# The passage between two decoder layers: order of the last batch's work, places of seven products, and one turning moved by a slot

## The chip, the cores and the metric

One core of one Trainium2 chip runs the whole kernel. Its engines work side by side, each through its own queue in order: TensorE (PE, with its weight loads shown as PEld), VectorE (DVE), ScalarE (ACT), GpSimd (POOL) and SyncE (SP), whose queue issues most transfers. An instruction that waits for another engine holds up everything behind it in its own queue. The metric is the device time of one execution in microseconds (us), lower is better.

## The reference

Two decoder layers over 32 batches of 100 tokens with 256 features, 16 heads of 16. Each layer is self-attention, cross-attention to 361 context rows per batch, and a feed-forward part, each followed by a residual and a normalisation without weights. All is in float32. Cut to what matters here:

```python
x = layernorm(x + L0_attn(x))                      # adds x once more inside
x = layernorm(x + L0_xattn(x, ctx, ctx, dist))     # scores - |scale| * log(dist + 1e-9)
x = layernorm(x + L0_ffn(x))
x = layernorm(x + L1_attn(x))
x = layernorm(x + L1_xattn(x, ctx, ctx))
x = layernorm(x + L1_ffn(x))                       # router, the best of 8 experts, times its share

def L0_ffn(x):
    xn = (x - mean) * rsqrt(var + 0.001) * ln_gamma + ln_beta
    w_q = clip(round(weight / (mean(abs(weight)) + EPS)), -1, 1)
    gamma = max(abs(xn))                           # over ALL batches and tokens
    xq = clip(xn * 128 / gamma, -128 + EPS, 128 - EPS)
    return (xq @ w_q) * (gamma * beta / 128)
```

The maximum `gamma` is taken over all batches. So the feed-forward part of layer 0, and with it all of layer 1, can start only when the last batch has passed layer 0's cross-attention.

## The kernel before

The attention part of both layers is one program written by hand in slots. `at(slot, place, do)` files a step under a slot and a place; `run_slots` then walks the slots in order and records every step, which fixes the order in each engine's queue. No scheduler moves anything afterwards.

A slot `s` consists of the scores of the unit two slots ahead (TensorE into the four score banks, then `centre` on DVE and POOL), place -1 and place 0, and then three turns of the unit one slot ahead (TensorE transposes the centred scores, ACT takes the exponential out of PSUM), each followed by places 1, 2 and 3. Last come the sums of the slot's own unit (weights times values). A unit is the self-attention of a batch or a quarter (four heads) of its cross-attention: five units, so five slots, per batch. There is only one set of score banks, so the next unit's scores wait until DVE has read the last ones. All other products go through four PSUM banks in turn, `bank(...)`.

Layer 0's cross-attention of batch b starts in slot 5b, so the last one, batch 31, in slot 155. Layer 1's starts in slot 183 + 5b, and its self-attention earlier: batches 0 to 3 in slots 173, 175, 177 and 179, batch 4 in slot 185. Between slots 160 and 182 lies what is called the passage here.

The last batch's chain in the passage: `normalised` (the transposes `r_n_x`, then on DVE a reciprocal and the product `o_x`), the turning of `o_x` (`r_x_ox`), `residual` (product `r_o_x`, then on DVE the sum and its statistics, on POOL the power -0.5), `centre_and_scale`, `layer_norm_scale`, `feed_forward_input` (`xn` and its largest magnitude into `absmax`), then `scale_of_all` in slot 164, place 3: a reduction of `absmax` on DVE, a transpose `r_gmax`, another reduction, a product `r_gamma` that spreads the result over 128 partitions, and the scales. `clipped` then makes `xq`, and `feed_forward` (`r_f`) gives the first rows of layer 1.

Beside it the passage makes 34 pieces. For each of batches 2 to 9 (`AHEAD`) three value products of layer 1's cross-attention (`r_v_ahead`, each two matmuls and an ACT copy) are made ahead into a stage and stored to DRAM; for batches 0 and 1 there are two key pieces (`r_k`) and three value pieces (`r_v`) each. `PASSAGE` lists the slot and place of each piece in this order. Behind the last piece of a batch SP issues the store of its values and the load of the context for the batch two further on.

For a batch of layer 1 from 4 on, self-attention has its scores in slot `early` - 2 and its sums in slot `late` = `early` + 1. In slot `late` + 1 follow `normalised` at place 0 (`r_n_s`, then `o_s` on DVE) and the turning of `o_s` at place 3 (`r_x_os`, two transposes, and an ACT copy). In slot `late` + 2 that copy goes into `residual` at place 2 (`r_o_s`). That slot begins with the scores of the next batch's self-attention.

Of the kernel before, what the change touches and what calls it, by code (L numbers as in the profile page):

```python
# [16 lines left out]
B, S, D, H, DH = 32, 100, 256, 16, 16  # L17
# [17 lines left out]
NO_TOKEN = 1000000  # L35
ROUND = 12582912.0
AHEAD = range(2, 10)
PASSAGE = ((160, 3), (160, 3), (160, 3), (161, 1), (162, 2), (162, 2), (163, 1), (163, 2), (163, 2), (163, 3), (164, 1), (164, 1),
           (164, 2), (165, 1), (166, 1), (167, 3), (167, 3), (167, 3), (169, 1), (169, 3), (171, 3), (171, 3), (173, 1),
           (174, -1), (174, 0), (175, 1), (176, -1), (176, 0), (177, 1), (178, -1), (178, 0), (179, 1), (180, -1), (180, 0))  # L40
LAYER = (0, SLOTS * B + 23)
COLUMNS = ("parity", "steps", "l0s_bq", "l0s_bk", "l0s_bv", "l0x_bq", "l0x_bk", "l0x_bv", "l1x_bq", "l1x_bk", "l1x_bv")
ROWS = ((("l0s_bo", D), ("l0x_bo", D), ("dscale", 1), ("ffn_g", D), ("ffn_b", D)),
# [21 lines left out]
def decoder_kernel(ctx: ExitStack, tc: tile.TileContext, a: dict, out: bass.AP):  # L65
# [7 lines left out]
    xnT = state.tile([P, NC2, B, S], F32, name="xnT")  # L73
# [7 lines left out]
    def layer_norm_scale(pool, src, eps, kind, tag):  # L81

        n = src.shape[0]
        st = pool.tile([n, 6], F32, tag="ln_st", name=f"st_{tag}")
        nc.vector.bn_stats(st, src)
        mv = pool.tile([n, 2], F32, tag=f"ln_mv_{kind}", name=f"mv_{tag}")
        nc.vector.bn_aggr(mv, st)  # L87
        rs = pool.tile([n, 1], F32, tag=f"ln_rs_{kind}", name=f"rs_{tag}")
        nc.gpsimd.tensor_scalar_add(rs, mv[:, 1:2], eps)  # L89
        nc.gpsimd.tensor_tensor(rs, rs, mhalf[:n], ALU.pow)  # L90
        return mv[:, 0:1], rs

    def centre_and_scale(dst, src, scale):
        nc.vector.tensor_scalar(dst, src, scale[0], scale[1], ALU.subtract, ALU.mult)

    with ExitStack() as att:
# [7 lines left out]
        def bank(tag):  # L104
            return ps_r.tile([P, 512], F32, tag="r", name=f"r_{tag}")

        def split(t, n):
            return t.rearrange("p (n s) -> p n s", n=n)
# [129 lines left out]
        def transpose_rows(src, kind, tag, dst=None):  # L238

            ps = bank(f"x_{kind}{tag}")[:, :NC2 * S]  # L240
            for k in range(NC2):
                nc.tensor.transpose(ps[:, k * S:(k + 1) * S], src[:, k * P:(k + 1) * P], ident[:S, :S])
            if dst is None:
                dst = w2.tile([P, NC2, S], F32, tag=f"xT_{kind}", name=f"xT_{kind}{tag}")
            nc.scalar.copy(dst, split(ps, NC2))
            return dst
# [35 lines left out]
        def normalised(avs, tag):  # L282


            psn = bank(f"n_{tag}")[:S].rearrange("p (h r) -> p h r", r=32)
            for g in range(NG):
                nc.tensor.transpose(psn[:, g * NG:(g + 1) * NG, :].rearrange("p h r -> p (h r)"), avs[:, g, :], ident)
            rc = sm.tile([S, H], F32, tag="rc", name=f"rc_{tag}")
            nc.vector.reciprocal(rc, psn[:, :, DH])
            o = w2.tile([S, H, DH], F32, tag="o", name=f"o_{tag}")  # L290
            nc.vector.tensor_tensor(o, psn[:, :, :DH], rc.unsqueeze(2).to_broadcast([S, H, DH]), ALU.mult)
            return o
# [6 lines left out]
        def residual(oT, w_o, y, weight, kind, tag):  # L299

            pso = bank(f"o_{kind}{tag}")[:S, :D]
            for k in range(NC2):
                nc.tensor.matmul(pso, lhsT=oT[:, k, :], rhs=w_o[:, k, :], start=(k == 0), stop=(k == NC2 - 1))
            nc.vector.scalar_tensor_tensor(y, y, weight, pso, ALU.mult, ALU.add)
            return layer_norm_scale(sm, y, 1e-05, kind, f"{kind}{tag}")
# [91 lines left out]
        def at(slot, place, do):  # L397
            plan.setdefault((slot, place), []).append(do)
# [68 lines left out]
        def starts(l, b):  # L467


            return LAYER[l] + SLOTS * b, LAYER[l] + (2 * b - 10 if b < 4 else SLOTS * (b - 4) + 2)  # L470
# [20 lines left out]
        def plan_passage():  # L491
# [17 lines left out]
            for load, of_batch in [ahead(b) for b in AHEAD] + [(live[1, b]["load"], live[1, b]["pieces"]) for b in range(2)]:  # L509
                n = len(loads)  # L510
                loads.append(load)
                pieces += [(f, None) for f in of_batch[:-1]] + [(of_batch[-1], n + 2)]
            assert len(pieces) == len(PASSAGE)
            for i in range(2):
                at(157 + i, 0, loads[i])
                at(157, 3, lambda i=i: nc.gpsimd.memset(stage[i][:, :, :, DH:], 1.0))
            for (slot, place), (f, then) in zip(PASSAGE, pieces):
                at(slot, place, f)
# [3 lines left out]
        def plan_batch(l, b):  # L522
            start, early = starts(l, b)
            t = live[l, b] = {}
            sx = f"l{l}x"
            tag = f"{l}_{b}"

            def keep(key, f):
                def do():
                    t[key] = f()  # L530
                return do
# [52 lines left out]
            def flat(o):  # L584
                return o.rearrange("p h d -> p (h d)")
# [24 lines left out]
            late = early + (b > 3)  # L610
            bursts.setdefault(late, []).append(steps[early].sums)
            at(early if b < 4 else early - 2, 0, keep("y_s", lambda: add_share(c[f"l{l}s_bo"], "s", b, tag)))
            at(late + 1, 0, keep("o_s", lambda: normalised(t["av_s"], f"s{tag}")))
            at(late + 1, 3, keep("oT_s", lambda: transpose_rows(flat(t["o_s"]), "os", tag)))
            at(late + 2, 2, keep("ln_s", lambda: residual(t["oT_s"], c[f"l{l}s_wo"], t["y_s"], 1.0 if l else 2.0, "s", tag)))
            at(late + 3, 2, lambda: centre_and_scale(xs[b], t["y_s"], t["ln_s"]))
            for g in range(NG):
# [6 lines left out]
            at(start + 7, 1, keep("ln_x", lambda: residual(t["oT_x"], c[sx + "_wo"], t["y_x"], 1.0, "x", tag)))  # L624
            at(start + 8, 1, lambda: centre_and_scale(xs[b], t["y_x"], t["ln_x"]))
            if l == 0:
                at(start + 8, 2, keep("ln_n", lambda: layer_norm_scale(sm, xs[b], 0.001, "n", f"n_{b}")))
                at(start + 9, 3, feed_forward_input)
                at(start + 11, 3, lambda: transpose_rows(t["xn"], "n", tag, dst=xnT[:, :, b, :]))
            else:  # L630
                at(start + 9, 0, keep("x3T", lambda: transpose_rows(xs[b], "m", tag)))
                first, n = group_of(b)
                r, steps_of_group = ROUTING[max(0, b - (B - 3))]
                at(start + r[0], r[1], router)
                if b == first + n - 1:
                    for do, (s, place) in zip((ranked, exponentials, ahead_of, counted, shares, rows_of), steps_of_group):
                        at(start + s, place, lambda do=do: do(first, n))
                    s, place = steps_of_group[-1]
                    for i in range(n):
                        at(start + s + i, place, lambda i=i: send(first + i))  # L640
# [9 lines left out]
        def group_of(b):  # L650

            if b >= B - 2:
                return b, 1
            first = b // GROUP * GROUP
            return first, min(GROUP, B - 2 - first)
# [51 lines left out]
        def send(b):  # L707
            nc.gpsimd.tensor_copy(place[:, b:b + 1], row[:, b:b + 1])
            scatter("regions", out=regions, out_offset=bass.IndirectOffsetOnAxis(ap=place[:, b:b + 1], axis=0),
                    in_=x_all[:, b, :])  # L710
# [97 lines left out]
        for l in range(2):  # L808
            for b in range(B):
                plan_batch(l, b)  # L810
            for b in range(0, B, 2):
                plan_pair(l, b)
# [196 lines left out]
```

## Time and profile before

| | us |
|---|---|
| median of 3 runs (lowest, highest) | 1762.18 (1759.08, 1764.57) |
| the profiled execution | 1765.71 |
| its span, first to last instruction | 1763.7 |
| layer 0, to the end of the last batch's `r_n_x` | 0 to 834.27 |
| passage, to layer 1's first cross-attention scores | 834.27 to 906.04 |
| start of layer 1's cross-attention, to batch 1's second scores | 906.04 to 934.02 |
| rest of layer 1 | 934.02 to 1664.30 |
| experts | 1664.30 to 1763.7 |
| granted TensorE clock, mean over the span | 0.986 of full |

Every row of an engine's timeline is one or more instructions of the same line that ran behind each other: the start, the time from the first start to the last end, the engine, the line of the kernel, the tiles written and read, and the count. In brackets stands how long the engine had been idle before it and what ended the wait. A product of two matmuls in float32 appears as four matmul records. Consecutive rows overlap by some 0.16 us, since the end of a matmul overlaps the start of the next, so costs are taken from start to start. Tiles that begin with `r_` are the PSUM banks of a product, `sc_` the score banks; buffer and batch numbers are left out of the names.

### The profile page before, as it was taken

How to read it: one execution, taken by the hardware profiler on the slowest of the kernel's cores; microseconds unless marked ns; L12 is line 12 of the kernel's file. 1: busy time of each engine (PE TensorE's matmuls, PEld its weight loads, DVE VectorE, ACT ScalarE, POOL GpSimd, SP SyncE). 2: the span in 40 equal slices, each digit the busy share in tenths (PEclk: the TensorE clock that was granted, in tenths of full speed). 3: DMA queues.
4: the chain of work that ended last, by engine and by line, in shares of the span. 5: the costliest groups of instructions: out<-in, count | busy, mean ns of one | idle time of the engine just before them, and what ended most of it. 6: DMA issues, size and time to landing. Idle time of an engine off the chain costs nothing. (4 is left out here: it accounts for less than half of the span.)

```text
span 1763.7 us, 52249 instructions
## 1 busy us (share of the span) xinstructions
PE 1691.6 (96%) x20801; PEld 1307.2 (74%) x20801; DVE 1292.9 (73%) x3784; ACT 910.5 (52%) x2252; POOL 1098.6 (62%) x1657
## 2 busy tenths in 40 slices
PE   7999999999999999999899999999999999999786
PEld 6777777777777777766667777777777777777575
DVE  4677777777778777777567887877768787777655
ACT  3455555555555555555445555555555555554354
POOL 1566666666666666666136668776767667775646
PEclk9999999999999999999999999999999999999888
DMA  4001332333233223200601132000000000010083
GB/s 153 20 21 30 80 76 52 84 80 76 56 84 81 71 57 84 76 25 22 209 20 46 54 102 64 19 20 19 28 19 15 24 19 28 31 32 18 18 249 117
DMA packets 64047, 104.90 MB, mean 59 GB/s; under 512 B 6107, under 2 KB 43485, under 8 KB 63678
## 3 DMA queue, kind: packets, MB, share of 16 engines
q1 hardware_dynamic: 59790, 94.44, 19.2%
q0 software_dynamic: 3584, 6.59, 1.2%
q8 instruction: 165, 2.70, 0.6%
q14 instruction: 76, 0.62, 0.1%
q10 hardware_dynamic: 432, 0.54, 0.1%
HBM read 61.32 MB, written 41.13 MB: 58 GB/s over the span
## 5 line engine op out<-in xcount | busy, mean ns | idle before, releaser
L364 POOL TENSOR_TENSOR pr<-pr,mx_x 100x361 f32<-100x361 f32 x992 | 767.0, 803 | 230.9 <-DVE mx_x L360 222.2
L375 ACT ACTIVATE pT_x<-r_t_x 120x400 f32<-120x400 f32 (+1 forms) x768 | 371.8, 504 | 305.7 <-PE r_t_x L374 304.8
L374 PEld LDWEIGHTS r_t_x<-ident,pr 100*120 100x120 f32 (+1 forms) x3072 | 314.1, 138 | 119.0 <-POOL pr L364 39.5
L374 PE MATMUL r_t_x<-ident,pr 100*120 100x100 f32 (+1 forms) x3072 | 384.1, 253 | 14.5 <-POOL pr L364 12.7
L360 DVE CUSTOM_DVE_ANT_0 pr<-sc_x,dist 100x361 f32<-100x361 f32 x512 | 244.6, 531 | 122.7 <-PE sc_x L277 113.7
L360 DVE CUSTOM_DVE_ANT_0 pr<-sc_x,zero 100x361 f32<-100x361 f32 x512 | 244.6, 530 | 76.6 <-PE sc_x L277 65.6
L277 PE MATMUL sc_x<-kT_x,qz_x 32*100 32x361 f32 x2048 | 222.4, 503 | 8.3 <-DVE mx_x L360 5.2
L89 POOL TENSOR_SCALAR rs_s<-mv_s 100x1 f32<-100x1 f32 x64 | 14.4, 225 | 293.8 <-DVE mv_s L87 264.6
L389 PE MATMUL r_a_x<-pT_x,v_cross 120*32 120x100 f32 (+1 forms) x6144 | 172.7, 253 | 0.0
L318 DVE TENSOR_REDUCE mx_s<-sc_s 100x16 f32<-100x1600 f32 x64 | 116.7, 1823 | 75.0 <-PE sc_s L277 75.0
L477 ACT ACTIVATE kT_x<-r_k,c_columns 128x361 f32<-128x361 f32 x128 | 72.1, 564 | 162.4 <-PE r_k L475 162.4
L389 PEld LDWEIGHTS r_a_x<-pT_x,v_cross 120*32 120x32 f32 (+1 forms) x6144 | 130.2, 110 | 23.9 <-ACT kT_s L424 2.2
L332 ACT ACTIVATE pT_s<-r_t_s 100x400 f32<-100x400 f32 x256 | 112.9, 505 | 33.3 <-PE r_t_s L331 31.0
L321 DVE TENSOR_TENSOR pr_s<-sc_s,mx_s 100x1600 f32<-100x1600 f32 x64 | 116.8, 1825 | 2.2
L331 PE MATMUL r_t_s<-ident,pr_s 100*100 100x100 f32 x1024 | 107.3, 251 | 0.3 <-DVE pr_s L321 0.3
L277 PEld LDWEIGHTS sc_x<-kT_x,qz_x 32*100 32x100 f32 x2048 | 68.3, 160 | 45.9 <-issue 13.9
L484 PE MATMUL r_v<-shared,ctx 128*120 128x256 f32 (+1 forms) x384 | 100.4, 384 | 0.0
L331 PEld LDWEIGHTS r_t_s<-ident,pr_s 100*100 100x100 f32 x1024 | 95.1, 130 | 5.8 <-ACT shared L486 0.7
L486 ACT COPY v_cross<-r_v 120x256 f32<-120x256 f32 x168 | 62.6, 373 | 57.5 <-PE r_v L484 57.5
L268 DVE SCALAR_TENSOR_TENSOR qz_x<-r_qx,qm_x_scale,qm_x_bias 128x400 f32<-128x400 f32 x64 | 37.6, 629 | 72.7 <-PE r_qx L257 72.7
L475 PE MATMUL r_k<-ctx,shared 128*128 128x361 f32 x256 | 89.6, 472 | 1.1 <-DMA ctx<-in_ctxT_dram 1.1
L475 PE MATMUL r_k<-ctx,c_l1x_wk 128*128 128x361 f32 x256 | 89.2, 471 | 0.0
(220 smaller groups left out, 2920.2 us busy)
## 6 DMA issues: line engine op xcount, KB each, us to landing
regions<-no_token SPq DMA_DIRECT2D x23, 1161.0 KB
ctx<-in_ctxT_dram SPq DMA_DIRECT2D x64, 361.0 KB
wb<-in_experts_dram SPq DMA_DIRECT2D x32, 257.0 KB
values_dram<-shared SPq DMA_DIRECT2D x8, 768.0 KB
v_cross<-values_dram SPq DMA_DIRECT2D x8, 768.0 KB
dist<-in_dist_dram SPq DMA_DIRECT2D x32, 141.0 KB
xb<-regions SPq DMA_DIRECT2D x32, 129.0 KB
x_all<-in_x_dram SPq DMA_DIRECT2D x32, 100.0 KB
```

Of the source, the lines that this page charges most:

```text
L277: nc.tensor.matmul(dst, lhsT=qz[rows, p, k, :], rhs=kT[rows, k, :], start=True, stop=True)
L318: nc.vector.tensor_reduce(mx, sg, AX.X, ALU.max)
L321: nc.vector.tensor_tensor(pr, sg, mx.unsqueeze(3).to_broadcast([S, NG, NG, S]), ALU.subtract)
L331: nc.tensor.transpose(pt[:, j, :], t["pr_s"][:, j, g, :], ident[:S, :S])
L332: nc.scalar.activation(t["pT_s"][:, g], pt, AF.Exp)
L360: nc.vector.tensor_tensor_reduce(pr[:, j, :SK], sc[:, j, :], bias, 1.0, LOWEST, ALU.add, ALU.max, mx)
L364: nc.gpsimd.tensor_tensor(pr[:, j, :SK], pr[:, j, :SK], mx.to_broadcast([S, SK]), ALU.subtract)
L374: nc.tensor.transpose(pt[:n, j, :], t["pr_x", g][:, j, k0:k0 + n], ident[:S, :S])
L375: nc.scalar.activation(t["pT_x", g][:n, i], pt[:n], AF.Exp)
L389: nc.tensor.matmul(av[32 * j:32 * j + 32, h, :], lhsT=t["v_x"][:n, i, head(part, j), :], rhs=t["pT_x", part][:n, i, j, :], start=(i == 0), ...
L475: nc.tensor.matmul(ps, lhsT=c[sx + "_wk"][:, k, m * P:(m + 1) * P], rhs=t["ctx"][:, k, :], start=(k == 0), stop=(k == NC2 - 1))
L484: nc.tensor.matmul(ps, lhsT=ctx_b[:, k, k0:k0 + n], rhs=c[sx + "_wv"][:, k, :], start=(k == 0), stop=(k == NC2 - 1))
```

## The change

Three edits, none of which alters a value that is computed:

- The places of the 34 pieces. Before, 13 of them stood in slots 160 to 164; now six do. From there on every piece takes a place that another had before, and the last seven go into slots 181 to 186, where there were none.
- For batch 30 alone (`b == B - 2`), `feed_forward_input` and the transposes of its result move two slots on, from 159 to 161 and from 161 to 163. On DVE its three instructions thereby come behind `o_x` of batch 31.
- For batches 4 to 31 of layer 1, the turning of `o_s` moves from place 3 of slot `late` + 1 to place -1 of the next. In PE's queue it now comes behind the sums of the slot and behind the 16 matmuls of the next batch's self-attention scores, ahead of the next turns.

```diff
-PASSAGE = ((160, 3), (160, 3), (160, 3), (161, 1), (162, 2), (162, 2), (163, 1), (163, 2), (163, 2), (163, 3), (164, 1), (164, 1),
-           (164, 2), (165, 1), (166, 1), (167, 3), (167, 3), (167, 3), (169, 1), (169, 3), (171, 3), (171, 3), (173, 1),
-           (174, -1), (174, 0), (175, 1), (176, -1), (176, 0), (177, 1), (178, -1), (178, 0), (179, 1), (180, -1), (180, 0))
+PASSAGE = ((160, 3), (161, 1), (162, 2), (162, 2), (163, 1), (163, 2), (165, 1), (166, 1), (167, 3), (167, 3), (167, 3),
+           (169, 1), (169, 3), (171, 3), (171, 3), (173, 1), (174, -1), (174, 0), (175, 1), (176, -1), (176, 0), (177, 1),
+           (178, -1), (178, 0), (179, 1), (180, -1), (180, 0), (181, 3), (182, 0), (182, 2), (183, 0), (183, 3), (185, 3), (186, 0))
...
-            at(late + 1, 3, keep("oT_s", lambda: transpose_rows(flat(t["o_s"]), "os", tag)))
+            at(*((late + 2, -1) if l and b > 3 else (late + 1, 3)), keep("oT_s", lambda: transpose_rows(flat(t["o_s"]), "os", tag)))
...
             if l == 0:
+                wait = 2 * (b == B - 2)
                 at(start + 8, 2, keep("ln_n", lambda: layer_norm_scale(sm, xs[b], 0.001, "n", f"n_{b}")))
-                at(start + 9, 3, feed_forward_input)
-                at(start + 11, 3, lambda: transpose_rows(t["xn"], "n", tag, dst=xnT[:, :, b, :]))
+                at(start + 9 + wait, 3, feed_forward_input)
+                at(start + 11 + wait, 3, lambda: transpose_rows(t["xn"], "n", tag, dst=xnT[:, :, b, :]))
```

## The prediction

> **What bounds the kernel now.** I read the page first: engine totals, then the slices. TensorE is busy for 96% of the span, and in the slices it stands at 9 tenths nearly everywhere; only the two ends fall lower at full width. So time is to be had where TensorE waits, or where its clock is cut.
>
> ```profile
> PE 1691.6 (96%) x20801; PEld 1307.2 (74%) x20801; DVE 1292.9 (73%) x3784; ACT 910.5 (52%) x2252; POOL 1098.6 (62%) x1657
> ```
>
> Then the busy time by stretch, for the stages in the table above (columns after the length: busy time and count of PE, PEld, DVE, ACT, POOL, then granted clock, DMA share, GB/s). The passage loses 71.77 - 65.61 = 6.2 us of TensorE, the next 28 us lose 4.6 us, and there the clock is 0.82. All of layer 1 after it loses 13.2 us in 730, 5.4 of them in its last 64.
>
> ```profile
> 834.27:906.04 71.77, 65.61 (x571) 51.18 (x570) 42.43 (x89) 29.02 (x76) 13.74 (x29) 1.00 0.41 135
> 906.04:934.02 27.98, 23.43 (x266) 17.64 (x265) 17.52 (x52) 10.94 (x27) 16.81 (x23) 0.82 0.05 14
> 934.02:1664.30 730.28, 717.08 (x9330) 544.47 (x9326) 558.11 (x1745) 381.15 (x933) 505.31 (x761) 1.00 0.11 33
> ```
>
> Third, the timeline of PE in the passage (start, us, engine, line, tiles, then the wait before it). The reader sees pieces (r_v_ahead, three per line of 12) standing ahead of r_gmax, two of them held by their loads, and r_o_x of the last batch late because o_x was late.
>
> ```profile
> 833.69 0.75 PE L287 MATMUL r_n_x<-ident,avs_x 128*100 128x128 f32 x4
> 834.27 2.77 PE L484 MATMUL r_v_ahead<-c_l1x_wv,ctx_ahead 128*120 128x256 f32 x12
> 838.32 0.36 PE L242 MATMUL r_x_ox<-ident,o_x 100*128 100x100 f32 x2 [1.28 <-DVE o_x L291]
> ...
> 839.75 1.03 PE L303 MATMUL r_o_x<-shared,xT_ox 128*100 128x256 f32 x4
> ...
> 847.95 2.82 PE L484 MATMUL r_v_ahead<-c_l1x_wv,ctx_ahead 128*120 128x256 f32 x12 [0.91 <-DMA ctx_ahead<-in_ctxT_dram]
> 852.50 1.09 PE L484 MATMUL r_v_ahead<-c_l1x_wv,ctx_ahead 128*120 128x256 f32 x4 [1.72 <-DMA ctx_ahead<-in_ctxT_dram]
> 853.43 0.27 PE L779 MATMUL r_gmax<-ident,gmax 128*1 128x128 f32 x1
> ...
> 856.44 1.89 PE L443 MATMUL r_f<-wq,xq 128*100 128x256 f32 x8
> ```
>
> Fourth, the same for DVE: batch 30's normalisation waits for POOL, and batch 31's r_n_x, done at 834.44, is taken at 837.47. The maximum itself is ready at 847.48, and r_gmax starts 5.95 us later.
>
> ```profile
> 836.24 0.85 DVE L572 SCALAR_TENSOR_TENSOR xn<-xn,rs_n,c_rows 100x256 f32<-100x256 f32 x1 [0.75 <-POOL rs_n L90]
> 837.13 0.42 DVE L573 TENSOR_REDUCE absmax<-xn 100x1 f32<-100x256 f32 x1
> 837.47 0.25 DVE L289 RECIPROCAL rc_x<-r_n_x 100x16 f32<-100x16 f32 x1
> ...
> 847.29 0.19 DVE L777 TENSOR_REDUCE gmax<-absmax 128x1 f32<-128x32 f32 x1
> ```
>
> Last, PE and its clock where cross-attention of layer 1 starts (stretch, length, busy and count, clock, DMA share, GB/s).
>
> ```profile
> 913.40:916.80 3.40, 1.29 (x10) 0.96 0.00 0
> 916.80:920.20 3.40, 3.32 (x19) 0.50 0.02 5
> 920.20:923.60 3.40, 3.40 (x16) 0.54 0.00 0
> ...
> 927.00:930.40 3.40, 1.87 (x16) 0.97 0.00 0
> 930.40:933.80 3.40, 3.40 (x61) 0.53 0.02 5
> ```
>
> A stretch with 38% busy and one with 55% are each followed by half clock: 6.8 us and 3.4 us of it, worth 10.2 / 2 = 5.1 us where TensorE is full.
>
> **The change, step by step** (in the clock of the profile before; pieces cost 0.87 us start to start, 2.77 for three with 0.16 of tail; a key piece 1.22, 877.55 to 878.77).
>
> *1. Batch 30's input moves two slots.* Its three DVE instructions (0.48, 0.85, 0.42) and its two transposes now stand behind batch 31's division. The division can start when st_n's aggregate ends, 834.97; o_x ends at 835.70 (0.28 + 0.42 as before). r_x_ox follows at 835.85 (0.15 as between 838.17 and 838.32), one piece behind it until 836.92, r_sum 0.14, so r_o_x at 837.06 instead of 839.75: 2.7 us earlier. The moved three fill DVE until 837.8, before r_o_x ends at 838.1: they hold up nothing, else they would cost their 1.75 us. From r_o_x to the maximum is DVE and POOL work of unchanged order, 840.78 to 847.48 = 6.7 us, so it is ready at 844.8.
>
> *2. Seven pieces leave the slots ahead of r_gmax.* Left between r_o_x and r_gmax are four pieces and the folds (0.86 + 0.22 + 0.87), then batch 30's transposes: TensorE is through at 843.6. It waits 1.3 us for the maximum, r_gmax 844.9; then 0.5 us to r_gamma, two pieces and batch 31's transposes as before; xq is ready at 847.3 and r_f starts at 847.9, against 856.44: 8.5 us earlier. It is 6.1 us of pieces gone, and waits of 4.4 us (1.28, 0.91, 1.72, 0.46) become 2.3 us (0.55, 1.3, 0.46). SP issues a store and a load per batch, and each load lands 4.5 us after its issue (843.41 to 847.95); the load of the next piece goes out at 839.9 and is there at 844.4, before its use at 846.
>
> *3. A load that becomes late.* The load of the fifth batch made ahead is issued behind the piece at (167, 3), now 851.6, so it lands at 856.1; the piece at (169, 3) is reached at 863.49 - 8.55 = 854.9. It waits about 1.1 us, and behind it in PE's queue stand batch 0's self scores: the lead falls to 7.5 us. (Bounds: 0, if a lone load is quicker, to 1.5.)
>
> *4. Slots 174 to 180* hold the same number of pieces, but two of the four key pieces are now value pieces: 2 x 0.35 = 0.7 us less. The first cross scores (906.04) come 8.2 us earlier.
>
> *5. Seven pieces arrive in slots 181 to 186*: five of 0.87 and two of 1.22 = 6.8 us, with their ACT copies (0.37, 0.56) on an engine that is 39% busy there. Walked through in the old clock: the two before the first turns move batch 4's self scores from 912.02 to 913.6 and cover the waits for POOL; two more and one behind those scores stand in the time that DVE needs for them (1.82 + 1.82), where TensorE stood 0.45 + 0.45 + 1.32 us; sc_x at 916.88 becomes 918.4 (0.7 us still idle). Five pieces have cost 1.55 us. With no stretch as empty as the one of 38%, the clock stays whole: from there to the next sc_x is 5.1 us instead of 8.3, which puts it at 923.6 instead of 925.19. The last two cover 0.96 and 0.57; sc_x at 934.02 comes at 930.4. Together 3.6 us earlier for 6.8 us more work.
>
> *6. The turning of o_s* (28 batches) moves behind the self scores. What it takes away is in its row:
>
> ```profile
> L242 PE MATMUL r_x_os<-ident,o_s 100*128 100x100 f32 x52 | 9.0, 254 | 0.8 <-ACT pT_x L375 0.4 <-DVE o_s L291 0.3
> ```
>
> The two transposes cost 0.26 us start to start in either place. Behind them on PE now stand the next turning (waiting for POOL 1.7 us in all of layer 1) and 2.4 us later r_o_s, which needs their copy on ACT (0.33): slack 2.0 us. I take -0.5 us, between -0.8 (its waits) and +1.1 (half of 28 times the 0.08 us by which the pitch of eight transposes differs beside it: 0.69 at 1217.68, 0.78 at 1212.86).
>
> Sum: -8.2 - 3.6 - 0.5 = -12.3 us. Against it I set +1.0: TensorE now waits 1.3 and 0.46 us close together around r_gmax, and 1.1 us at step 3; a stretch of 3.4 us at half clock costs 1.7, and I give it a little over one half. **-11.3 us.** Nothing takes it back: until 1664 TensorE is 98% full. The profiled execution took 1765.71 us (span 1763.7) and would take 1754.4; the median shown, 1762.18, is 3.5 us below that execution, so I predict **1751 us**.
>
> **Rivals.**
>
> *A. The clock does not follow small gaps.* Then covering 1.3 and 1.0 us of waits leaves the two cuts where they are, and 5.1 us of the sum go: -6.2, 1756. For it: a stretch of 65% (1657.5 to 1660.9) has no cut behind it and one of 73% has. Against: both cuts here begin within 0.1 us of an emptier stretch's end. The Trainium skill (TensorE: Matmul & The Clock Gate, "Why this matters for your kernels") asks only for no idle gaps over some 3 us between bursts; by that rule waits of 1.3 us are no cause, and the sum would be A's. The trace speaks against it: the longest wait before the cut at 916.8 is 1.32 us. Chance 0.14.
>
> *B. The cut moves into the thinned passage.* Around r_gmax (843.6 to 845.7) TensorE is now 1.8 us idle, and again at step 3. Two cuts of 6.8 us cost 6.8 us where I set 1.0: -5.5, 1756.7. Chance 0.14.
>
> *C. The pieces in slots 181 to 186 lie on the path.* If DVE and POOL keep pace with TensorE there, so that the scores slip by each piece, their 6.8 us are paid in full and the clock is still cut: -8.2 + 6.8 - 0.5 = -1.9, 1760. For it: POOL runs eight subtractions without a break from 926.86 to 933.1. Against: DVE waits for PE 3.3 us at 923.78. Chance 0.09.
>
> *D. Slower: the turning comes late.* In its new place it stands ahead of the next batch's turning in PE's queue. If r_o_s, or that turning, waited for it in each of 28 batches, the gain of 11.3 is gone from 0.40 us a batch; at 0.7 us it is +8, 1770. That needs r_o_s' 2.0 us of slack to be missed by as much, and only ACT's queue could do it (avs copy 0.24, then this copy). Chance 0.06.
>
> **How the numbers follow.** Forecast 0.57; A 0.14; B 0.14; C 0.09; D 0.06. A difference of 0.3% (5.3 us) is about what a measurement of this kernel can tell from none: faster is below 1756.9. The forecast, A and most of B lie there, with C outside: faster 0.81, same 0.12, slower 0.07. The range reaches down to 1746 (no cut at all, step 3 free, all of step 6's waits gone: -14 or so, and the runs' own spread of 3 us) and up to 1760, which takes in A, B and C's edge.
>
> **What would show it.** In the passage no piece ahead of r_gmax waits for a load; r_gmax itself waits for DVE and starts some 11.2 us behind r_n_x of batch 31 (19.7 before). The stretch from r_n_x's end to the first cross scores is 8 us shorter, that from there to batch 1's second scores 3 to 4 us shorter, at clock 1.00. Layer 1 after that is within 1 us of 730. A passage that gains less than 5 us, a cut clock in it, or waits before r_o_s would prove me wrong.

## The result, and the profile after

| | before | changed | ratio (95% interval) |
|---|---|---|---|
| median of 6 runs each, us | 1763.08 | 1751.59 | 0.9938 (0.9924 to 0.9952) |
| lowest to highest | 1759.08 to 1764.93 | 1749.84 to 1752.99 | |
| profiled execution (its span) | 1765.71 (1763.7) | 1752.82 (1750.9) | |

The kernel became 11.5 us faster. The spans of the two profiles differ by 12.8 us. Cut at the same instructions, so that the parts add up:

| stretch | before | after | difference | forecast |
|---|---|---|---|---|
| start to `r_n_x` of batch 31 | 833.69 | 833.55 | -0.14 | 0 |
| to the first cross scores of layer 1 | 72.35 | 65.13 | -7.2 | -8.2 (steps 1 to 4) |
| to batch 1's second scores | 27.98 | 25.16 | -2.8 | -3.6 (step 5) |
| to batch 31's self scores | 631.79 | 628.07 | -3.7 | -0.5 (step 6) |
| to the first expert block | 114.79 | 115.99 | +1.2 | 0 |
| to the end | 83.10 | 83.0 | -0.1 | 0 |

The stretches of the changed kernel (length, then busy time and count of PE, PEld, DVE, ACT, POOL, clock, DMA share, GB/s). The second has TensorE busy for 24.5 of 25.2 us at full clock, where 23.4 of 28.0 were busy at 0.82.

```profile
834.14:898.68 64.54, 58.33 (x542) 46.12 (x541) 42.17 (x89) 26.24 (x69) 13.42 (x29) 1.00 0.43 145
898.68:923.84 25.16, 24.51 (x294) 18.17 (x293) 17.46 (x52) 12.97 (x34) 16.13 (x23) 1.00 0.11 30
923.84:1651.50 727.66, 716.24 (x9329) 544.99 (x9326) 556.88 (x1743) 383.27 (x933) 505.39 (x762) 1.00 0.11 33
```

PE's timeline in the passage after the change (start, us, instruction, the wait before it). `r_o_x` starts 3.25 us behind `r_n_x` instead of 6.06, `r_gmax` waits for DVE and no longer for loads, and `r_f` starts 14.2 us behind `r_n_x` instead of 22.75. The last line is the load that came late.

```profile
833.55 0.75 PE L287 MATMUL r_n_x<-ident,avs_x 128*100 128x128 f32 x4
834.14 1.04 PE L484 MATMUL r_v_ahead<-c_l1x_wv,ctx_ahead 128*120 128x256 f32 x4
835.58 0.36 PE L242 MATMUL r_x_ox<-ident,o_x 100*128 100x100 f32 x2 [0.40 <-DVE o_x L291]
...
836.80 1.09 PE L303 MATMUL r_o_x<-shared,xT_ox 128*100 128x256 f32 x4
...
844.74 0.27 PE L780 MATMUL r_gmax<-ident,gmax 128*1 128x128 f32 x1 [1.27 <-DVE gmax L778]
...
847.75 1.89 PE L443 MATMUL r_f<-wq,xq 128*100 128x256 f32 x8
...
857.02 1.09 PE L484 MATMUL r_v_ahead<-c_l1x_wv,ctx_ahead 128*120 128x256 f32 x4 [2.40 <-DMA ctx_ahead<-in_ctxT_dram]
```

DVE's timeline there: the division is taken as soon as the statistics before it are through, and batch 30's input no longer stands ahead of it.

```profile
834.75 0.23 DVE L289 RECIPROCAL rc_x<-r_n_x 100x16 f32<-100x16 f32 x1
...
836.77 0.48 DVE L572 SCALAR_TENSOR_TENSOR xn<-xn,rs_n,c_rows 100x256 f32<-100x256 f32 x1
...
844.40 0.19 DVE L778 TENSOR_REDUCE gmax<-absmax 128x1 f32<-128x32 f32 x1
```

And the row of the moved turning among the groups of layer 1. Its own waits are gone; the 0.8 us that it had were not what the move was worth.

```profile
L242 PE MATMUL r_x_os<-ident,o_s 100*128 100x100 f32 x50 | 9.8, 277 | 0.0
```

### The profile page after: what moved, and what is told of

It is laid out like the page before. It is cut to its first block, busy times and chain, and to the rows that moved or that the text cites. A ratio compares the mean times of both kernels' runs of the same rounds, so it can differ in the third digit from the quotient of the medians.

```text
span 1750.9 us, 52238 instructions
## 1 busy us (share of the span) xinstructions
PE 1684.7 (96%) x20801; PEld 1303.6 (74%) x20801; DVE 1291.1 (74%) x3784; ACT 913.0 (52%) x2252; POOL 1096.9 (63%) x1657
```

## The experiments

Three groups of runs, each measured beside the kernel before on one chip: places, input, turning and filled; then load first, both layers, places and input, and the first of the two runs of all together; then the last two. A "cut" is a stretch in which TensorE is granted half its clock. In the table "passage" is from `r_n_x` of batch 31 to the first cross scores, "start of layer 1" from there to batch 1's second scores, both from the profile.

### Each edit alone

```diff
-PASSAGE = ((160, 3), (160, 3), (160, 3), (161, 1), (162, 2), (162, 2), (163, 1), (163, 2), (163, 2), (163, 3), (164, 1), (164, 1),
...
+PASSAGE = ((160, 3), (161, 1), (162, 2), (162, 2), (163, 1), (163, 2), (165, 1), (166, 1), (167, 3), (167, 3), (167, 3),
...
```

> The kernel before with the new list of places alone. Theory (the three edits earn in three different stretches): batch 31's division still stands behind batch 30's input, so the product r_o_x stays within 0.3 us of its old place, but r_gmax then waits for DVE and not for loads, and r_f of batch 0 starts about 6 us earlier than before (8.5 with all edits). The stretch from the first cross scores to batch 1's second scores is about 2.8 us shorter with the clock at 1.00. In all about 7.5 us less than before (ratio 0.9957). Rival (the gain at r_f comes from the earlier division alone, the pieces were hidden anyway): no more than 3.5 us less.

```diff
+                wait = 2 * (b == B - 2)
...
-                at(start + 9, 3, feed_forward_input)
+                at(start + 9 + wait, 3, feed_forward_input)
...
```

> The kernel before with batch 30's input two slots later alone. Theory: o_x and r_o_x come 2.5 us earlier, and the maximum is ready 2.5 us earlier, but r_gmax still stands behind thirteen pieces and their loads, so r_f of batch 0 moves by less than 1 us: -1 to 0 us in all, nothing that can be measured. Rival (the chain through the division sets the passage by itself): 2.5 us less.

```diff
-            at(late + 1, 3, keep("oT_s", lambda: transpose_rows(flat(t["o_s"]), "os", tag)))
+            at(*((late + 2, -1) if l and b > 3 else (late + 1, 3)), keep("oT_s", lambda: transpose_rows(flat(t["o_s"]), "os", tag)))
```

> The kernel before with the turning of o_s moved alone. Theory from the two traces (each pair of batches of layer 1 saves 0.19 us on PE, since the two transposes stand in a wait that no row names): 3.6 us less by batch 31's self scores, about 1 us given back behind them, 2.5 us less in all (ratio 0.9986). Rival (the prediction's step 6: worth 0.5 us, and the rest of layer 1's gain came from the earlier start of the layer): 0.5 us less, no gain from batch to batch.

The first two edits together, without the third:

> The first two edits together, without the turning. Theory (the two need each other: alone the places leave a 3 us wait for the division in which the clock is cut, alone the earlier division only meets the loads): r_f of batch 0 8.5 us earlier than before, no cut of the clock in the passage, and 8.4 us less than before in all (1753.7, ratio 0.9952), far more than the -3.3 and +1.8 of the two alone. Rival (they add up): 1.5 us less, 1760.6.

| kernel | median, runs | before beside it | ratio (95% interval) | `r_n_x` to `r_f` | passage | start of layer 1 |
|---|---|---|---|---|---|---|
| before | | | | 22.75 | 72.35 | 27.98 |
| places alone | 1758.8, 12 | 1762.13 | 0.9983 (0.9973 to 0.9993) | 18.52 | 70.14 | 25.15 |
| input alone | 1763.95, 12 | 1762.13 | 1.0009 (1.0000 to 1.0019) | 25.45 | 75.05 | 24.91 |
| turning alone | 1760.01, 12 | 1762.13 | 0.9982 (0.9969 to 0.9995) | 22.77 | 72.37 | 24.91 |
| places and input | 1754.83, 5 | 1764.46 | 0.9941 (0.9927 to 0.9955) | 14.20 | 65.40 | 25.15 |
| all three | 1751.59, 6 | 1763.08 | 0.9938 (0.9924 to 0.9952) | 14.19 | 65.13 | 25.16 |

Places alone: `r_f` was expected 6 us earlier and came 4.2 earlier, and the whole 3.3 us instead of 7.5. That is within the rival's bound of 3.5, but not for its reason: `r_f` came earlier without an earlier division, and `r_o_x` even came 1.1 us later (7.15 us behind `r_n_x`, 6.06 before). PE's timeline of that kernel shows what stood against the gain. With fewer pieces and the division still late, TensorE waited 3.00 us:

```profile
836.44 0.36 PE L242 MATMUL r_x_ox<-ident,o_x 100*128 100x100 f32 x2 [3.00 <-DVE o_x L291]
836.64 1.88 PE L484 MATMUL r_v_ahead<-c_l1x_wv,ctx_ahead 128*120 128x256 f32 x4
```

and its stretches of 3.4 us (length, PE's busy time and count, clock, DMA share, GB/s) show the clock at one half behind that wait. The piece, the sum and batch 30's transposes in it took twice their time. A second cut stands behind the late load (from 860.6).

```profile
833.50:836.90 3.40, 0.46 (x3) 0.97 0.00 0
836.90:840.30 3.40, 3.40 (x12) 0.53 0.00 0
```

Input alone: `r_o_x` came 1.7 us earlier, and `r_f` 2.7 us later. The pieces met their loads sooner, and from the end of the wait of 2.73 us on the clock was cut for 6.8 us (the two pieces ahead of `r_f` took 3.53 us instead of 1.99), as PE's timeline of that kernel shows. The expected "nothing" lies at the edge of its interval; a gain of 2.5 us is excluded.

```profile
842.13 2.82 PE L484 MATMUL r_v_ahead<-c_l1x_wv,ctx_ahead 128*120 128x256 f32 x12 [1.24 <-DMA ctx_ahead<-in_ctxT_dram]
...
850.47 2.03 PE L484 MATMUL r_v_ahead<-c_l1x_wv,ctx_ahead 128*120 128x256 f32 x4 [2.73 <-DMA ctx_ahead<-in_ctxT_dram]
...
853.65 3.53 PE L484 MATMUL r_v_ahead<-c_l1x_wv,ctx_ahead 128*120 128x256 f32 x8
```

So the two do not add up: -3.3 and +1.8 us alone, -9.6 together (1764.46 to 1754.83), as the theory for both had it (-8.4; the rival's -1.5 is outside the interval), though the profile of both shows one cut of 3.4 us, behind the late load, where the theory had none. In the profiles `r_f` moves by -4.2 and +2.7 us alone and by -8.55 together. An estimate from the rows in the cuts: ahead of `r_f` the cut in the places alone cost about 1.6 us (`r_x_ox` to the end of `r_o_x`), and that in the input alone about 2.8 (the piece ahead of `r_gmax` to `r_f`). Without them `r_f` would have moved by some -5.8 and -0.1, near what was expected. So of the 7.0 us by which the two together do better than their sum, some 4.4 are cuts behind the waits that either alone leaves. The other 2.6 are the queues: an earlier division gains little while thirteen pieces and their loads stand ahead of `r_gmax`, and fewer pieces gain more when the division is there.

Turning alone: 2.1 us, near the expected 2.5. From batch 1's second scores to batch 31's self scores it takes 628.22 us, against 631.79 before, 631.81 with the first two edits and 628.07 with all three. The 3.6 us belong to the turning alone; an earlier start of the layer gives nothing there.

### Added products in the gaps

```diff
+            def fill_bank():
+                ps = bank("idle")[:120, :D]
+                for k in range(NC2):
+                    nc.tensor.matmul(ps, lhsT=c["l1x_wv"][:, k, :120], rhs=c["l1x_wv"][:, k, :], start=(k == 0), stop=(k == NC2 - 1))
+
+            for slot, place in ((181, 3), (182, 0), (182, 2), (183, 0), (183, 3), (185, 3), (186, 0)):
+                at(slot, place, fill_bank)
```

> The kernel before with seven added products of a value piece's size (0.87 us each, 6.1 us in all), written to a PSUM bank that nobody reads, at the places in slots 181 to 186 where the change puts its last pieces. Theory (the waits there empty TensorE so far that its clock is cut in half): the waits of 4.5 us are mostly filled, the clock stays at 1.00, and the stretch from the first cross scores to batch 1's second scores takes 24.5 us or so instead of 28: 3 to 4 us less than before though 6.1 us of work are added. Rival A (the clock does not follow small waits): both cuts stay, and the kernel takes 1.5 us more; if DVE sets the pace there as well (rival C) up to 6 us more.

Measured: 1760.89 us (12 runs) beside 1762.13, ratio 0.9998 (0.9990 to 1.0007). 6.1 us of products cost nothing. The stretch itself went as expected, 24.70 us at full clock; the filled kernel's start of layer 1, with the columns of the stretches of the changed kernel above:

```profile
903.67:928.37 24.70, 23.79 (x293) 18.09 (x292) 17.45 (x52) 10.45 (x27) 16.12 (x23) 1.00 0.06 16
```

The whole did not fall by the expected 3 to 4 us. As far as the profiles show, the reason is that the profiled execution of before had much of the cut: 10.2 us of half clock in that stretch. Two other profiles without pieces there (input alone, turning alone) had 3.4 us of it, and took 24.91. So the cut varies from one execution to the next. In the profile of the filled kernel it is gone, and its runs are narrower: the 12 of them lie within 2.1 us of each other (1760.07 to 1762.13), the 35 of the kernel before within 7.9 (1758.61 to 1766.53), the 12 of each of the three kernels above within 5.8 to 8.1. Of 12 profiles, the three without work in slots 181 to 186 all have a cut there, the nine with it none. Rivals A and C both asked for more time than before and fall.

### The late load, and a version with the waits taken out

```diff
                 at(slot, place, f)
                 if then is not None and then < len(loads):
                     at(slot, place, loads[then])
+                if store:
+                    at(slot, place, store)
```

> The changed kernel with SP's load of the next context put ahead of the store of the values made ahead. Theory (step 3 was under-sized because the store and the next pair share the DMA engines with the load: landed 5.6 us after its issue): the load of the fifth batch lands some 3 us after its issue, the wait of 2.4 us at the piece in (169, 3) falls under 0.5 us, and the kernel takes about 2 us less than the changed one (ratio to before 0.993). Rival (the load is slow by itself): no change, 0.994.

Measured: 1750.43 us (5 runs) beside 1764.46, ratio 0.9916 (0.9902 to 0.9929). By the times alone it is not shown to be faster than the changed kernel, whose interval (0.9924 to 0.9952) overlaps. The traces show that the wait is gone: the piece in (169, 3) waits no more, and from `r_f` to batch 0's self scores it takes 7.66 us instead of 10.30. In this profile the passage is only 0.75 us shorter, since the waits around `r_gmax` brought a cut of 3.4 us, which the changed kernel's profile had not: the pieces behind it took 3.67 us instead of 1.99, in PE's timeline of this kernel:

```profile
845.07 0.27 PE L783 MATMUL r_gmax<-ident,gmax 128*1 128x128 f32 x1 [1.27 <-DVE gmax L781]
845.81 0.35 PE L786 MATMUL r_gamma<-gmax,ones 1*128 1x1 f32 x2 [0.47 <-DVE gmax L784]
846.08 3.67 PE L484 MATMUL r_v_ahead<-c_l1x_wv,ctx_ahead 128*120 128x256 f32 x8
```

Then the turning in layer 0 too:

```diff
-            at(*((late + 2, -1) if l and b > 3 else (late + 1, 3)), keep("oT_s", lambda: transpose_rows(flat(t["o_s"]), "os", tag)))
+            at(*((late + 2, -1) if b > 3 else (late + 1, 3)), keep("oT_s", lambda: transpose_rows(flat(t["o_s"]), "os", tag)))
```

> The changed kernel with the turning of o_s moved for batches 4 to 31 of layer 0 as well. Theory (the move itself costs 0.05 us a batch and earns only where a wait for POOL stands behind its new place, which layer 1 shows once in two batches): layer 0 lists such waits too (r_t_x for POOL 6.6 us in 19 places), so 0 to 2 us less than the changed kernel. Rival (the new place is better by itself): 3 us less.

1752.51 us (5 runs) beside 1764.46, ratio 0.9931 (0.9918 to 0.9945). From batch 6's to batch 31's self scores layer 0 takes 629.60 us, against 630.01 in the changed kernel: 0.4 us, against 3.4 for the same batches of layer 1 (605.53 to 602.09). The new place is not better by itself.

All of it together, with a piece more ahead of `r_gmax` and one ahead of batch 3's rows:

```diff
-PASSAGE = ((160, 3), (161, 1), (162, 2), (162, 2), (163, 1), (163, 2), (165, 1), (166, 1), (167, 3), (167, 3), (167, 3),
-           (169, 1), (169, 3), (171, 3), (171, 3), (173, 1), (174, -1),
...
+PASSAGE = ((160, 3), (161, 1), (162, 2), (162, 2), (163, 1), (163, 2), (163, 3), (165, 1), (166, 1), (167, 3), (167, 3), (167, 3),
+           (169, 1), (169, 3), (171, 3), (171, 3), (173, -1), (174, -1),
...
```

> The changed kernel with four more moves: load ahead of store, the turning moved in both layers, one piece more ahead of r_gmax (at slot 163, place 3, so that each later piece takes the place of the one before it and the place at 186 falls away), and the piece of slot 173 at place -1, ahead of the turning of batch 3's rows that waits 1.07 us. By the traces: 2.0 for the load, 0.9 of the 1.3 us wait for the maximum, 0.9 of the 1.07, 0 to 2 for the turning: 4 to 5 us less than the changed kernel (about 1747, ratio to before 0.9914). Rival (the waits move on to the next load or to DVE): no more than 2 us less.

> The changed kernel itself, as the measure for the next one on the same chip. Theory: ratio to before 0.993 to 0.994; in its profile a cut of the clock of 3.4 us may stand behind the wait for the load (as with e6 and e8) or not (as in the first profile), which moves it by 1.5 us.

> The kernel of e7 beside the changed one on one chip. Theory (its waits are gone: 2.4 us for the load, 0.9 for the maximum, 0.6 for batch 3's rows, and with them the cut): 3 to 5 us less than the changed kernel. Rival (chips differ, the gap is the chip's): within 2 us of it.

First 1747.7 us (4 runs) beside 1764.46, ratio 0.9903 (0.9887 to 0.9918); then, on one chip, 1749.2 (6 runs) and the changed kernel 1750.52 (6 runs) beside 1763.01, ratios 0.9921 (0.9903 to 0.9940) and 0.9933 (0.9914 to 0.9953). In the two profiles of that pair the passage is 2.5 us shorter (62.59 against 65.13) and the time from `r_n_x` to the end 3.9 us (914.04 against 917.95). The medians differ by 1.3 us, not by the 3 to 5 that were expected, and the intervals overlap; the rival's "within 2 us" is what the times show. That this version beats the changed kernel is likely by the traces and not shown by the times.

## Why the prediction was right, and where its steps were not

The forecast was 11.3 us less, 1751 us, and the kernel took 1751.59, 11.5 less. The instants of the passage were right to 0.1 us up to `r_f`, so the mechanism there held. That the sum came so close is in part luck. Between the two profiles, 12.8 us apart, step 6 brought 3.2 us more than its term and the 1.0 us set aside for a cut was not needed; against that the passage gained 1.0 less, step 5 gained 0.8 less, and 1.2 were lost ahead of the experts.

- Steps 1 and 2 held. Counted from `r_n_x`, `r_o_x` was forecast at 3.37 us and came at 3.25, `r_gmax` at 11.21 and 11.18, `r_f` at 14.21 and 14.19. The moved input covered nothing and held up nothing. That either edit alone is worth so little was not in the prediction.
- Step 3 named the right load, but its wait is 2.4 us, not 1.1, outside the 1.5 that the step gave as its bound. The load was issued at 851.42 and used at 857.02, 5.6 us later and not 4.5. The next pair, a store at 854.42 and a load at 854.84, was issued while the first was still under way. With the loads put ahead of the stores the wait is gone; how much of it the later pair took, and how much the store ahead, was not separated.
- Step 4 said 0.7 us; from batch 0's self scores to the first cross scores the profile shows 1.0 (41.60 to 40.64).
- Step 5 was right in kind and 0.8 us too large against the same profile: the three parts came to +1.85, -3.10 and -1.57 us (forecast +1.55, -3.2 and -1.95). But its second part is the cut clock, which the profile of before had more of than the two others without pieces there. Against those (24.91 us) the 25.16 of the changed kernel are no gain at all: the seven pieces cost about nothing in their new places, and what they earn is that they left the old ones. The prediction's readings there were a little off as well: the cuts begin 0.27 and 0.22 us ahead of the ends of its two emptier stretches (it says within 0.1), and the 3.41 us right ahead of the first are 45% busy, not 38%.
- Step 6 failed in size: "I take -0.5 us, between -0.8 (its waits) and +1.1". It brought 3.7. From batch 13 on the two transposes cost 0.17 us or so less where they were taken out and 0.23 more where they were put in, so the move itself costs some 0.05 us a batch. But in three of four batches the whole 0.23 us is taken up behind the new place, mostly by waits so short that no row names them: for POOL in one of the three, for DVE in the two others. One of the latter, in batch 28 before the change:

```profile
1496.20 0.51 PE L374 MATMUL r_t_x<-ident,pr 100*122 100x100 f32 x4
1496.81 0.87 PE L277 MATMUL sc_x<-kT_x,qz_x 32*100 32x361 f32 x8
```

The scores start 0.61 us behind the first of the four transposes; after the change, where the transposes start 0.17 us later in the batch, it is 0.44 (1483.00 to 1483.44). From batch 26's to batch 27's self scores, PE alone (length, busy time and count, clock, DMA share, GB/s):

```profile
1442.27:1466.88 24.61, 24.48 (x323) 1.00 0.10 29
```

before, and after

```profile
1429.09:1453.51 24.42, 24.40 (x322) 1.00 0.10 29
```

while the next batch, one of the fourth kind, takes 25.16 us in both. From batch 12's self scores to batch 31's fifteen batches save 0.15 to 0.19 us each and four next to nothing, 2.7 us in all; batches 5 to 11 save another 0.9. So the 0.19 us for each pair of batches, from which the turning alone was expected, was too little: it is about 0.54 in four batches.

- The 1.0 us set against the sum for a cut in the passage was the right kind of term. The two profiles of the changed kernel show none, but three kernels with the same passage up to there had one: behind `r_gmax` (load first), and behind the late load (places and input, turning in both layers). The first cost 1.7 us, as priced. The two others cost 1.5 us at first, but the wait of 1.07 us for batch 3's rows behind them then fell away, so the passage is only 0.2 to 0.3 us longer than in the changed kernel (65.35 and 65.40 against 65.13). Rival B's two cuts of 6.8 us did not come.
- The 1.2 us lost before the experts is not the change's. The stretch from batch 31's self scores to the first expert block goes with the length of the cut at the end of layer 1: in the six profiles where it lasted 27.3 us the stretch took 116.0 to 116.2, in the six where it lasted 17.1 to 23.9 it took 114.3 to 114.8, and kernels with and without the moved turning are in both groups.

Of the rivals, the nine profiles without a cut in slots 181 to 186 speak against A, the filled kernel against C, and the turning alone against D. The Trainium skill's advice to leave no idle gap of more than some 3 us (TensorE: Matmul & The Clock Gate, "Why this matters for your kernels") was too mild a bound in this trace: cuts followed stretches of 3.4 us in which the longest wait was 1.27 or 1.32 us.

## What to carry to other kernels

Where one queue is full and another is late, look for both halves of the fix before judging either: taking filler out of TensorE's queue, and bringing the late chain forward, were worth 3.3 us and less than nothing alone, and 9.6 us together. Work that a busy stretch does not need there was free in a stretch with many short waits, where it also kept the clock whole, so try it there. The waits that a page lists by group are a lower bound: the move of an instruction that repeats 28 times was worth several times its own listed wait, because what stood behind its new place in the queue had been waiting too.

## What the runs showed of the hardware

- In each of the twelve profiles TensorE's clock changes only at instants that lie whole multiples of 3.413 us apart. In the kernel before, for example, the cuts begin at 916.53 and 930.18 us, four such steps apart, and last 6.83 and 3.41 us. From execution to execution this grid lies differently against the instructions.
- The cuts follow steps of the grid in which TensorE was about half busy or less, some of them without any long wait: 49% with waits of 1.27 and 0.47 us (load first, around `r_gmax`), 45% with none over 1.32 (before, from 913.12). Between 20 and 1636 us of the twelve profiles, all eight steps under 48.5% at full clock were followed by a cut, three of the eight between 49% and 59%, and none above that. At the end of layer 1, behind 1636 us, a step of 73% (all together, second run) was followed by one as well, so the busy share alone does not decide it. Two steps of the kernel with the load first (length, PE's busy time and count, clock, DMA share, GB/s); the first is followed by the second:

```profile
842.70:846.10 3.40, 1.66 (x11) 1.00 0.65 182
846.10:849.50 3.40, 3.40 (x9) 0.50 0.61 252
```

- So whether a wait brings a cut seems to depend on where it falls on the grid. The wait for the late load was 2.40 us in the changed kernel and 2.39 in that with places and input, with the same instructions around it. In the first, 52% of the step were busy and no cut followed; in the second 46%, and one did. That the step's share is the cause is argued from such pairs and not shown: around `r_gmax` 49% brought a cut with the load first and none in the second profile of the changed kernel. The changed kernel (columns as above):

```profile
855.39:858.81 3.42, 1.79 (x36) 1.00 0.96 325
858.81:862.22 3.41, 3.41 (x26) 1.00 0.01 3
```

and with places and input

```profile
855.81:859.22 3.41, 1.56 (x27) 1.00 1.01 341
859.22:862.63 3.41, 3.41 (x27) 0.50 0.06 23
```

- Nine of the twelve profiles are of the same code up to `r_n_x` of batch 31, but for batch 30's input (in the other three the turning is moved in layer 0 too). `r_n_x` came between 831.30 and 834.19 us, and the self scores of batch 6, early in it, already lie 2.8 us apart (107.39 to 110.17); from there all nine take 723.9 to 724.0. So the start is a noise of its own, about as large as the effects of two of the three edits, and the stretches above are counted from `r_n_x` for that reason. What makes it was not asked.
